# Four gated layers of cross attention and experts: routing by ScalarE, limits behind maxima, weights in the context's place, projections one ahead, two batches' keys first

## The chip, the cores and the metric

The kernel runs on one core of a Trainium2 chip. The metric is the device time of one execution in microseconds. A core has five engines with instruction queues of their own: TensorE (PE; PEld is its weight load), VectorE (DVE), ScalarE (ACT), GpSimd (POOL) and SyncE (SP), which here only issues DMAs. Each executes its queue in order; they meet through semaphores. Data lie in SBUF and PSUM with 128 partitions.

## The reference

`x` has 8 batches of 256 tokens of width 256, the context 8 batches of 256 tokens of width 192. Four layers each add a gated cross attention and a gated feed-forward part, on a layer norm of `x`:

```python
x = x + tanh(g_xattn[l]) * XATTN_l(layernorm(x), ctx)
x = x + tanh(g_ffn[l])   * FFN_l(layernorm(x))
```

- L0: the cosine of projected tokens and context in place of an attention; a feed-forward part in which only expert 0 counts.
- L1: softmax attention with 16 heads of 16, rows of padded tokens masked. FFN: 8 experts, each token takes its two best by gate logits (softmax over the two); `silu(x W1) * (x W2)` of width 682, then `W3`.
- L2: softmax attention with 16 heads of 64, then `w_o`. FFN: top 2 of 8 experts of width 256 by softmax scores plus a bias, and two shared experts.
- L3: 16 heads of 16 with clamped logits, `where(any(isnan(attn)), 1/Nkv, attn)`, then `Wo`:

```python
attn = einsum('bhqd,bhkd->bhqk', q, k) * scale
attn = softmax(clip(attn, -10000, 10000))
attn = where(any(isnan(attn)), 1.0 / Nkv, attn)
x = einsum('bhqk,bhkd->bqhd', attn, v) @ Wo + bo
```

  FFN: self attention over 256 tokens, in which a key mask splits tokens into two groups by their likeness to a guide vector; then a projection.

## The kernel before

The residual `x` stays in SBUF for the whole launch as 16 tiles of 128 tokens. The instruction order on each engine is made by the framework's scheduler at build time from the order in which the Python code issues operations; `behind(kind)` holds the next ones behind the last operation recorded under `latest[kind]`. PSUM is split in three large tiles (`psum2`, 2 x 512 floats) and two small ones (`psum1`).

**16-head attention** (`attention16`, in L1, L3 and L3's self attention). Work goes over batches b and four groups g of four heads. For a group, `greatest` makes logits (`lg`, eight matmuls of 32 rows in two `psum2` tiles) and their negated maxima over keys (`nms`, L641), with a clamp in L3 (L645). Every second group, `shift` transposes the maxima (`nt`) and adds them to the spare rows of the queries (L655). Three groups after `greatest`, `weights` makes the logits again, transposed and shifted (`lb`), and takes their exponential by ScalarE (`ex`; L1512 in L3). L3 then has `limits` (`limited`, L1518), by which VectorE clamps each exponential from below and above; the lower bound `low` of a half batch comes from ScalarE (`lowest`) and a broadcast DMA through DRAM. The limits are issued one group after the exponentials, and `values`, which multiplies the exponentials with the values, one group after that; `finish` transposes the result back. The next batch's `prologue` is a generator whose parts run beside these groups: mixing in the experts' results of the layer before (`x`, L1101), keys, values, norm (`xn`, L226), transposes (`xt`), queries. All loops are written in this order:

```python
                greatest(b, g)
            if late and 0 <= n - lag - 1 < n_all:
                limits(*divmod(n - lag - 1, 4))
```

After L3's attention, `copy_predicated` puts the mean in where a NaN was seen, and `out_projection` per batch transposes (`l3oNt`), copies by ScalarE (`l3oNT`, L762), multiplies with `Wo` (L769, in a `psum1` tile) and adds to `x` (L776).

**64-head-width attention** (`attention64`, L2) works in pairs of heads, with logits, exponentials, division, transposes (`et`) and values; `prologue(b)` makes batch b's mix, keys (`pk`), values (`pv`), norm and queries, four parts before the next batch's first pair.

**Experts.** `places` makes a list of tokens by expert from the mask of chosen experts. Each token has two places; slots hold 128 tokens of one expert, 39 slots in all. VectorE counts per expert (`own_n`, `run`, scan), TensorE sums over partitions (`pr`), VectorE gets places (`two`), then one-hot rows and columns (`row`, L966; `col`, L950; `what`, L955 and L958), TensorE multiplies them (`pi`, L971) and `token` (L977) is the list; `expert` is each slot's expert. `two_gates` picks the two gate weights of each token. `routed` then runs over slots: an indirect DMA gathers 128 tokens (`xg`, L1023), TensorE transposes them (`xt`, L1033), `value_load` puts the expert in a register, `first_half` multiplies with `w1` and `w2` (`ph`, L1129), `hidden_T` transposes the hidden layer (`ht`, L1050), `second_half` multiplies with `w3` (`po`, L1147). The weights of L1 take 17 MB in SBUF in three tiles: `l1_w1` is loaded early, `l1_w2` (5.5 MB) takes the place of earlier layers' weights (`w01_stack`) after L1's attention, `l1_w3` (6.1 MB in two DMAs) comes after it. Results go to DRAM by slot and are gathered back for each batch in the next layer's prologue (`combined`).

Of the kernel before, what the change touches and what calls it, by code (L numbers as in the profile page):

```python
# [15 lines left out]
P = 128  # L16
# [4 lines left out]
E = 8  # L21
# [14 lines left out]
def flamingo_kernel(ctx: ExitStack, tc: tile.TileContext, out: bass.AP, a: dict):  # L36
# [112 lines left out]
    def rows_of_halves(k, name, value=1.0):  # L149
# [9 lines left out]
    trip = const.tile([P, P], F32, name="trip")  # L159
    nc.gpsimd.memset(trip, 1.0)  # L160
    nc.gpsimd.affine_select(
        out=trip, in_=trip, compare_op=ALU.is_gt, fill=0.0, base=0,
        pattern=[[1, P]], channel_multiplier=-1,
# [216 lines left out]
    maxima = cleared_maxima(l1x1, "l1")  # L380

    def rows(b, k):

        if b == 0:
            return l1x1.tile([P, 4, S], F32, name=f"l1{k}0")
        return l1x.tile([P, 4, S], F32, tag=f"{k}T", bufs=3, name=f"l1{k}{b}")

    def l1_prologue(b):

        cx = ctx01[:, :, b * S : (b + 1) * S]  # L390
        with behind("maxima") if b else nullcontext():
            xn = layer_norm(b, f"l1x{b}", rowmask=maskf[:, 2 * b : 2 * b + 2])
        qT = rows(b, "q")
        kT = rows(b, "k")
        for _, pp in project(wk, 2, lambda c: cx[:, c, :], 2, f"l1pk{b}"):
            for u in range(2):
                nc.scalar.activation(
                    of_half(kT, u), pp[:, 0:2, :], AF.Identity,
                    bias=one_a[:, u : u + 1], scale=half[:, u : u + 1],
                )  # L400
        yield
        xnT = lnp.tile([P, 2, S], F32, tag="xnT", name=f"xnT_l1x{b}")
        transposed(xn, xnT, f"l1x{b}")
        yield
        for _, pp in project(wq, 2, lambda c: xnT[:, c, :], 2, f"l1pq{b}"):
            for u in range(2):
                nc.vector.tensor_scalar(
                    of_half(qT, u), pp[:, 0:2, :], quarter[:, u : u + 1], None, ALU.mult
                )
        yield  # L410
        va = vas[b % 3]
        values16(wv, lambda c, k: cx[:, c, k * P : (k + 1) * P], va, f"l1pv{b}")
        yield qT, kT, va

# [91 lines left out]

    def attention64(tag, pl, prologue, epilogue, lag=2):

# [72 lines left out]

        gens[0] = prologue(0)
        while 0 not in state:
            advance(0)
        for n in range(n_all + lag + 1):
            if n < n_all:
                b, p = divmod(n, npair)
                if p == 0 and b + 1 < B:
                    gens[b + 1] = prologue(b + 1)
                logits(b, p)  # L590
                advance(b + 1)
# [6 lines left out]
    def attention16(tag, pl, maxima, prologue, epilogue, mrow=16, lag=3, clamp=None,  # L598
# [73 lines left out]
        def limits(b, g):  # L672
            for p in (2 * g, 2 * g + 1):
                clamp[2](b, p, exs[b, p])
# [47 lines left out]
        for n in range(n_all + lag + 1 + late):  # L722
# [5 lines left out]
            if late and 0 <= n - lag - 1 < n_all:  # L728
                limits(*divmod(n - lag - 1, 4))
            if n < n_all:  # L730
# [16 lines left out]

    def out_projection(att, nf, w, gate, brow, b, pl, name, bufs=1):

        projected(out_transposed(att, nf, pl, name, bufs), nf, w, gate, brow, b, name)  # L750

    def out_transposed(att, nf, pl, name, bufs=1):
# [11 lines left out]

    def projected(attT, nf, w, gate, brow, b, name):
        po = psum1(f"{name}o")
        for i in range(2):
# [127 lines left out]

    w01_stack.close()


    def places(mask, name, pl1, kept):

        flat = mask.rearrange("p e t -> p (e t)")
        run = pl1.tile([P, E * NT], F32, name=f"{name}run")
        nc.vector.tensor_tensor_scan(run, ones[:, : E * NT], flat, 0.0, ALU.mult, ALU.add)
        nc.vector.tensor_sub(run, run, flat)
        own_n = pl1.tile([P, E], F32, name=f"{name}own_n")
        nc.vector.tensor_reduce(own_n, mask, AX.X, ALU.add)
        pr = psum1(f"{name}pr")
        nc.tensor.matmul(pr[:, P : P + E], ones, own_n, start=True, stop=True)  # L910
        nc.tensor.matmul(pr[:, 0:P], trip, flat, start=True, stop=False)
# [3 lines left out]
        n_i = pl1.tile([P, E], I32, name=f"{name}n_i")  # L915
        nc.vector.tensor_scalar_add(n_i, pr[:, P : P + E], float(P - 1))
        nc.vector.tensor_single_scalar(n_i, n_i, -P, ALU.bitwise_and)
        sizes = pl1.tile([P, 2, E], F32, name=f"{name}sizes")
        nc.vector.tensor_copy(sizes[:, 0, :], n_i)
        nc.vector.tensor_sub(sizes[:, 1, :], sizes[:, 0, :], pr[:, P : P + E])  # L920
        lower = pl1.tile([P, 2, E, E], F32, name=f"{name}lower")
# [32 lines left out]
        what = pl1.tile([P, 2 * NT, 2, SP], BF16, name=f"{name}what")  # L954
        nc.vector.tensor_scalar_mul(what[:, :, 0, :], col, own_p)  # L955
        for k in range(2):
            ts = slice(k * NT, (k + 1) * NT)
            nc.vector.tensor_tensor(  # L958
                what[:, ts, 1, :], col[:, ts, :],
                count[:, :NT].unsqueeze(2).to_broadcast([P, NT, SP]), ALU.mult,  # L960
            )
        pi = psum1(f"{name}pi")
        for k in range(4):
            ts = slice(k * NT // 2, (k + 1) * NT // 2)
            row = pl1.tile([P, NT // 2, P], BF16, tag=f"{name}row", name=f"{name}row{k}", bufs=2)
            nc.vector.tensor_tensor(  # L966
                row, count.unsqueeze(1).to_broadcast([P, NT // 2, P]),
                rc[:, 0, ts].unsqueeze(2).to_broadcast([P, NT // 2, P]), ALU.is_equal,
            )
            for t in range(k * NT // 2, (k + 1) * NT // 2):  # L970
# [3 lines left out]
                )  # L974
        part = pl1.tile([P, SP], F32, name=f"{name}part")
        nc.vector.tensor_copy(part, pi[:, 0:SP])
        nc.vector.scalar_tensor_tensor(token, pi[:, SP : 2 * SP], float(P), part, ALU.mult, ALU.add)  # L977

        at = pl1.tile([P, SP, E], F32, name=f"{name}at")
        edge = pl1.tile([P, E], F32, name=f"{name}edge")  # L980
        nc.vector.tensor_scalar_mul(edge, first[:, 0, :], 1.0 / P)
        nc.vector.tensor_tensor(
            at, edge.unsqueeze(1).to_broadcast([P, SP, E]),
            count[:, :SP].unsqueeze(2).to_broadcast([P, SP, E]), ALU.is_le,
        )
        expert_f = pl1.tile([P, SP], F32, name=f"{name}expert_f")
        nc.vector.tensor_reduce(expert_f, at, AX.X, ALU.add)
        nc.vector.tensor_scalar_add(expert, expert_f, -1.0)
        return slot, two
# [25 lines left out]

    def routed(xd, yd, token, expert, first_half, second_half, nf, pl, name, halfway=None):

# [3 lines left out]
        def gather(s):  # L1021
            xg = pl.tile([P, D], F32, tag="xg", name=f"{name}xg{s}", bufs=4)
            nc.gpsimd.indirect_dma_start(  # L1023
# [86 lines left out]
    with tc.tile_pool(name="l1w", bufs=1, side="right") as plw:  # L1110
        l1_w2 = plw.tile([P, E, 2, HID], F32, name="l1_w2")
        nc.sync.dma_start(out=l1_w2, in_=a["l1f_w12"][:, :, :, HID:])
        l1_w3 = plw.tile([P, E, NHC, D], F32, name="l1_w3")
        for e0 in range(0, E, 4):
            nc.sync.dma_start(out=l1_w3[:, e0 : e0 + 4], in_=a["l1f_w3"][:, e0 : e0 + 4])
        l1_w12 = (l1_w1, l1_w2)
        token, expert, two_i, g2 = l1_kept
        with tc.tile_pool(name="l1p", bufs=1, side="right") as plp:
            slot, two = places(l1_mask, "l1g", plp, l1_kept[:3])
            l1_gates(slice(NT - 2, NT), "l1g_last")  # L1120
            two_gates(l1_gate, slot, two, gf(1), g2, "l1g", plp)
        with tc.tile_pool(name="l1f", bufs=2, side="right") as pl:
# [30 lines left out]
            def halfway():  # L1153
# [6 lines left out]
            routed(  # L1160
                l1xd, l1yd, token, expert, first_half, second_half, NHC, pl, "l1", halfway
            )


# [4 lines left out]
    with l2x_pool, tc.tile_pool(name="l2x", bufs=2) as pl:  # L1169
# [62 lines left out]

        attention64("l2", pl, prologue, epilogue)

# [6 lines left out]
    with tc.tile_pool(name="l2r", bufs=1) as pl1, ExitStack() as l2s_stack:  # L1241
# [18 lines left out]
        with tc.tile_pool(name="l2p", bufs=1) as plp:  # L1260
            slot, two = places(mask2, "l2g", plp, l2_kept[:3])
            nc.vector.tensor_tensor(gate2, gate2, mask2.rearrange("p e t -> p t e"), ALU.mult)
            two_gates(gate2, slot, two, gf(2), g2, "l2g", plp)

# [73 lines left out]
        with tc.tile_pool(name="l2f", bufs=2) as pl:  # L1338
# [60 lines left out]

            routed(xd, yd, token, expert, first_half, second_half, 2, pl, "l2")  # L1400
    l2w_stack.close()
# [3 lines left out]
    with tc.tile_pool(name="l3x", bufs=2) as pl, tc.tile_pool(name="l3x1", bufs=1) as pl1:  # L1405
# [31 lines left out]
        def prologue(b):  # L1437
# [27 lines left out]
            values16(wv3, lambda c, k: cx[:, c, k * P : (k + 1) * P], va, f"l3pv{b}")  # L1465
            xn = norm_apply(b, stats, f"l3x{b}")
            xnT = lnp.tile([P, 2, S], F32, tag="xnT", name=f"xnT_l3x{b}")
            transposed(xn, xnT, f"l3x{b}")
            yield
            pm = psum1(f"l3pm{b}")  # L1470
# [64 lines left out]
        nc.vector.tensor_copy(bad_i, bad_all.to_broadcast([P, D]))  # L1535
        for b in range(B):
            for i in range(2):
                nc.vector.copy_predicated(atts[:, 2 * b + i, :], bad_i, vmean[:, b, :])
            out_projection(atts[:, 2 * b : 2 * b + 2, :], 2, wo3, gx(3), None, b, pl, f"l3o{b}", bufs=2)

# [319 lines left out]
```

## Time and profile before

| | |
|---|---|
| median of 3 runs | 2044.46 us (2040.42 to 2046.01) |
| profiled execution | 2039.29 us, its span 2037.6 us |
| mean granted TensorE clock | 0.96 |
| L1 attention | 197 to 395 us of the span |
| L1 routing, up to the first gathered slot | 395 to 433 |
| L1 experts | 433 to 772 |
| L2 attention, its start included | 772 to 1206 |
| L2 router, shared experts, routing, experts | 1206 to 1447 |
| L3 attention, out-projections | 1447 to 1726, 1726 to 1755 |
| L3 self attention | 1755 to 2037.6 |

The profile is of one execution. A line of a group gives source line, engine, operation, output and inputs, count, then busy time and mean duration of one, then how long the engine had been idle just before these instructions and on what it waited. In a window's line each engine has its busy time and its instructions in brackets. Ends of matmuls are modelled, so sums of their durations overlap.

### The profile page before, as it was taken

Reading aid. Unit: us, or ns where it says so; the run is one execution under the profiler, and the core shown is the slowest. Engines: PE = TensorE matmul, PEld = TensorE weight load, DVE = VectorE, ACT = ScalarE, POOL = GpSimd, SP = SyncE. Lnnn points to the kernel's source line nnn. Section 1 sums busy time; section 2 is a strip of 40 time slices with the busy share of each in tenths; the row PEclk is TensorE's granted clock in tenths of the full one; section 3 lists DMA queues with packets and bytes.
Section 4 is the critical chain, followed back from the end, with each engine's and each line's share of the span. In section 5 each row is a group of like instructions: output and inputs, shape, how many; then the busy total and the mean of one; then the engine's idle time right before and its main releaser. Section 6 shows DMA issues by size and latency. Waiting matters only on the chain. (4 is left out here: it accounts for less than half of the span.)

```text
span 2037.6 us, 31056 instructions
## 1 busy us (share of the span) xinstructions
PE 1878.3 (92%) x12226; PEld 1237.3 (61%) x12226; DVE 1093.0 (54%) x2193; ACT 684.6 (34%) x1467; POOL 292.0 (14%) x324
## 2 busy tenths in 40 slices
PE   6999999859999998999999999999789898899998
PEld 5666666536666665566666665666555554675665
DVE  4534777631111113766666776333468777547763
ACT  2321444412221122433434432022254544234444
POOL 2421000011111101101111101033212110610000
PEclk8999999979999999999999999999889988999999
DMA  8000000151110114000000003023223221000000
GB/s 265 3 0 0 1 15 12 69 206 32 32 32 32 29 35 172 17 16 17 17 17 15 15 11 122 11 81 88 79 83 101 89 74 64 0 1 6 12 12 16
DMA packets 44285, 96.67 MB, mean 47 GB/s; under 512 B 6992, under 2 KB 30256, under 8 KB 40816
## 3 DMA queue, kind: packets, MB, share of 16 engines
q1 hardware_dynamic: 34736, 75.25, 10.4%
q0 software_dynamic: 6816, 18.62, 3.3%
q8 instruction: 100, 1.64, 0.3%
q10 hardware_dynamic: 2592, 0.82, 0.2%
q14 instruction: 41, 0.34, 0.1%
HBM read 78.02 MB, written 16.65 MB: 46 GB/s over the span
## 5 line engine op out<-in xcount | busy, mean ns | idle before, releaser
L1129 PE MATMUL l1ph<-l_w,l1xT 128*128 x624 | 191.0, 459 | 0.0
L537 ACT ACTIVATE l2ex<-l2lg,l2nm 128x256 f32<-128x256 f32 x256 | 118.1, 473 | 204.5 <-DVE l2nm L533 201.0
L1129 PEld LDWEIGHTS l1ph<-l_w,l1xT 128*128 128x128 f32 x624 | 115.9, 191 | 66.7 <-issue 13.6
L1139 DVE TENSOR_TENSOR l1h<-l1sl,l1ph 128x682 f32<-128x682 f32 x39 | 33.8, 866 | 175.1 <-PE l1ph L1129 170.3
L1147 PE MATMUL l1po<-l_w,l1hT 128*128 x468 | 121.1, 388 | 0.0
L1518 DVE SCALAR_TENSOR_TENSOR l3ex<-l3ex,l3low 128x1024 f32<-128x1024 f32 x64 | 75.8, 1225 | 49.7 <-ACT l3ex L1512 39.0
L641 DVE TENSOR_REDUCE l1nms<-l1lg 128x4 f32<-128x1024 f32 x64 | 75.5, 1221 | 43.7 <-PE l1lg L622 43.7
L641 DVE TENSOR_REDUCE l3nms<-l4lg 128x4 f32<-128x1024 f32 x64 | 75.4, 1220 | 40.2 <-PE l4lg L622 40.2
L1147 PEld LDWEIGHTS l1po<-l_w,l1hT 128*128 128x128 f32 x468 | 79.7, 189 | 19.8 <-issue 13.3
L533 DVE TENSOR_REDUCE l2nm<-l2lg 128x4 f32<-128x1024 f32 x64 | 78.0, 1219 | 21.3 <-PE l2lg L527 20.5
L1137 ACT ACTIVATE l1sl<-l1ph 128x682 f32<-128x682 f32 x39 | 28.9, 741 | 167.0 <-PE l1ph L1129 167.0
L557 DVE COPY l2et<-l2tp 128x512 f32<-128x512 f32 x128 | 83.4, 682 | 2.6 <-PE l2tp L553 2.5
L641 DVE TENSOR_REDUCE l3nms<-l3lg 128x4 f32<-128x1024 f32 x64 | 75.4, 1219 | 10.2 <-PE l3lg L622 10.1
L622 PE MATMUL l3lb<-l3q,l3k 32*128 32x256 f32 x512 | 63.9, 452 | 18.1 <-DVE l3nms L641 16.5
L542 DVE TENSOR_TENSOR l2ex<-l2ex,l2z 128x1024 f32<-128x1024 f32 x64 | 78.1, 1221 | 1.5
L1023 POOL DMA_INDIRECT l1xg<-l1xd,l1token x39 | 37.3, 956 | 282.1 <-PE l1xt L1033 255.3
L527 PE MATMUL l2lg<-l2k,l2q 64*128 64x256 f32 x512 | 76.5, 402 | 0.4 <-ACT l2ex L537 0.4
L1512 ACT ACTIVATE l3ex<-l3lb 128x1024 f32<-128x1024 f32 x64 | 64.8, 1018 | 34.3 <-PE l3lb L622 34.3
L667 ACT ACTIVATE l4ex<-l4lb 128x1024 f32<-128x1024 f32 x64 | 61.9, 1020 | 41.0 <-PE l4lb L622 40.6
L667 ACT ACTIVATE l1ex<-l1lb 128x1024 f32<-128x1024 f32 x64 | 62.0, 1022 | 40.1 <-PE l1lb L622 39.2
L572 PE MATMUL l2av<-l2et,l2va 128*32 128x256 f32 x1024 | 74.4, 385 | 0.0
L553 PE MATMUL l2tp<-ident,l2ex 128*128 128x128 f32 x512 | 71.2, 279 | 3.4 <-DVE l2et L557 2.8
(745 smaller groups left out, 3757.4 us busy)
## 6 DMA issues: line engine op xcount, KB each, us to landing
l3low<-low_d SPq DMA_DIRECT2D x16, 1024.0 KB
l_w<-in_l1f_w SPq DMA_DIRECT2D x2, 5456.0 KB
l_w<-in_l1f_w SPq DMA_DIRECT2D x2, 3072.0 KB
l1yd<-l1y SPq DMA_DIRECT2D x39, 128.0 KB
l2yd<-l2y SPq DMA_DIRECT2D x39, 128.0 KB
l_w<-in_l2f_w SPq DMA_DIRECT2D x1, 4096.0 KB
x<-in_x SPq DMA_DIRECT2D x8, 256.0 KB
w_l0f_w<-in_l0f_w SPq DMA_DIRECT2D x2, 1024.0 KB
```

What stands on the lines that cost most here:

```text
L527: nc.tensor.matmul(lg[:, j, i * S : (i + 1) * S], qT[r, p, i * P : (i + 1) * P], kT[r, p, :], start=True, stop=True,)
L533: latest["maxima"] = nc.vector.tensor_reduce(nm, lgv, AX.X, ALU.max, negate=True)
L537: nc.scalar.activation(ex[:, k, :], lgv[:, k, :], AF.Exp, bias=nm[:, k : k + 1], accum_out=z[:, k : k + 1],)
L542: nc.vector.tensor_tensor(ex, ex, z.unsqueeze(2).to_broadcast([P, 4, S]), ALU.mult)
L553: nc.tensor.transpose(tp[:, o : o + P], ex[:, 2 * j + i, k * P : (k + 1) * P], ident)
L557: nc.vector.tensor_copy(et, tp.rearrange("p (k n) -> p k n", k=2))
L572: nc.tensor.matmul(av[32 * j : 32 * j + 32, p % 4, :], va[:, k, 2 * p + j // 2, 32 * (j % 2) : 32 * (j % 2) + 32], pair[j // 2][:, k, :], ...
L641: latest["maxima"] = nc.vector.tensor_reduce(dst, lgv, AX.X, ALU.max, negate=True)
L667: nc.scalar.activation(exf, lbf, AF.Exp)
L1129: nc.tensor.matmul(ph[k][:, n, :HH], xT[:, c, :], l1_w12[k][:, bass.ds(e, 1), c, o : o + HH].rearrange("p o n -> p (o n)"), start=c == 0, ...
L1147: nc.tensor.matmul(po, hT[:n, f, :], l1_w3[:n, bass.ds(e, 1), f, :].rearrange("p o n -> p (o n)"), start=f == 0, stop=f == NHC - 1,)
L1518: nc.vector.scalar_tensor_tensor(exv, exv, 1.0, low.unsqueeze(1).to_broadcast([P, 2, 2 * S]), ALU.min, ALU.max)
```

## The change

- `places`: the count `own_n` is made first and gets a PSUM tile of its own (`pn`); `run - flat` goes into the constant `trip` (fill −1); ScalarE makes `what`, in 17 activations; `row` has four buffers; `token` is one reduction; the expert list is issued behind `token` (L1) or the rows (L2), and so are the gates.
- `l1_w2` is opened and loaded in the prologue of L1's last batch.
- `routed` takes the gathered tiles `xg` from a pool that is opened earlier.
- L1's rows of keys and queries have named tiles by `b % 3`.
- `attention64` can begin with four parts of batches 0 and 1 (`first_parts=4` in L2).
- In L3, `limits` is issued behind the maxima, `xn` too, and `xn`'s transposes one part later.
- L3's out-projections: batch b's transposes and copy are issued ahead of batch b−1's matmuls, whose result takes a `psum2` tile; the copies have three buffers.

```diff
@@ constants
-    nc.gpsimd.memset(trip, 1.0)
+    nc.gpsimd.memset(trip, 0.0)
     nc.gpsimd.affine_select(
-        out=trip, in_=trip, compare_op=ALU.is_gt, fill=0.0, base=0,
+        out=trip, in_=trip, compare_op=ALU.is_gt, fill=-1.0, base=0,
...
@@ l1_prologue(b)
         values16(wv, lambda c, k: cx[:, c, k * P : (k + 1) * P], va, f"l1pv{b}")
+        if b == B - 1:
+            w01_stack.close()
+            pool = l1w2_stack.enter_context(tc.tile_pool(name="l1w2", bufs=1, side="right"))
+            l1_w2.append(pool.tile([P, E, 2, HID], F32, name="l1_w2"))
+            nc.sync.dma_start(out=l1_w2[0], in_=a["l1f_w12"][:, :, :, HID:])
...
@@ attention64
-        gens[0] = prologue(0)
+        for b in range(2 if first_parts else 1):
+            gens[b] = prologue(b)
+            for _ in range(first_parts):
+                advance(b)
...
@@ attention16
             if late and 0 <= n - lag - 1 < n_all:
-                limits(*divmod(n - lag - 1, 4))
+                with behind("maxima"):
+                    limits(*divmod(n - lag - 1, 4))
...
@@ projected
-        po = psum1(f"{name}o")
+        po = psum2(f"{name}o")[:, 0, :] if wide else psum1(f"{name}o")
...
@@ places
+        own_n = pl1.tile([P, E], F32, name=f"{name}own_n")
+        nc.vector.tensor_reduce(own_n, mask, AX.X, ALU.add)
         run = pl1.tile([P, E * NT], F32, name=f"{name}run")
         nc.vector.tensor_tensor_scan(run, ones[:, : E * NT], flat, 0.0, ALU.mult, ALU.add)
-        nc.vector.tensor_sub(run, run, flat)
...
+        pn = psum1(f"{name}pn")
+        nc.tensor.matmul(pn[:, 0:E], ones, own_n, start=True, stop=True)
         pr = psum1(f"{name}pr")
-        nc.tensor.matmul(pr[:, P : P + E], ones, own_n, start=True, stop=True)
...
-        nc.vector.tensor_scalar_mul(what[:, :, 0, :], col, own_p)
-        for k in range(2):
-            ts = slice(k * NT, (k + 1) * NT)
-            nc.vector.tensor_tensor(
-                what[:, ts, 1, :], col[:, ts, :],
-                count[:, :NT].unsqueeze(2).to_broadcast([P, NT, SP]), ALU.mult,
-            )
+        nc.scalar.activation(what[:, :, 0, :], col, AF.Copy, scale=own_p)
+        what_t = what.rearrange("p (k t) w s -> p k t w s", k=2)
+        col_t = col.rearrange("p (k t) s -> p k t s", k=2)
+        for t in range(NT):
+            nc.scalar.activation(
+                what_t[:, :, t, 1, :], col_t[:, :, t, :], AF.Copy, scale=float(t * P)
+            )
...
-            row = pl1.tile([P, NT // 2, P], BF16, tag=f"{name}row", name=f"{name}row{k}", bufs=2)
-            nc.vector.tensor_tensor(
+            row = pl1.tile([P, NT // 2, P], BF16, tag=f"{name}row", name=f"{name}row{k}", bufs=4)
+            latest["rows"] = nc.vector.tensor_tensor(
...
-        part = pl1.tile([P, SP], F32, name=f"{name}part")
-        nc.vector.tensor_copy(part, pi[:, 0:SP])
-        nc.vector.scalar_tensor_tensor(token, pi[:, SP : 2 * SP], float(P), part, ALU.mult, ALU.add)
+            latest["token"] = nc.vector.tensor_reduce(
+                token, pi[:, : 2 * SP].rearrange("p (k s) -> p s k", k=2), AX.X, ALU.add
+            )
...
+        with behind(rest):
+            nc.vector.tensor_scalar_mul(edge, first[:, 0, :], 1.0 / P)
...
+            nc.vector.tensor_reduce(expert_f, at, AX.X, ALU.add)
+            nc.vector.tensor_scalar_add(expert, expert_f, -1.0)
...
@@ routed
-            xg = pl.tile([P, D], F32, tag="xg", name=f"{name}xg{s}", bufs=4)
+            xg = plg.tile([P, D], F32, tag="xg", name=f"{name}xg{s}", bufs=4)
...
@@ L1 experts
-            slot, two = places(l1_mask, "l1g", plp, l1_kept[:3])
-            l1_gates(slice(NT - 2, NT), "l1g_last")
-            two_gates(l1_gate, slot, two, gf(1), g2, "l1g", plp)
+            slot, two = places(l1_mask, "l1g", plp, l1_kept[:3], "token")
+            with behind("token"):
+                l1_gates(slice(NT - 2, NT), "l1g_last")
+                two_gates(l1_gate, slot, two, gf(1), g2, "l1g", plp)
...
@@ L2 attention, L2 experts
-        attention64("l2", pl, prologue, epilogue)
+        attention64("l2", pl, prologue, epilogue, first_parts=4)
...
-            slot, two = places(mask2, "l2g", plp, l2_kept[:3])
+            slot, two = places(mask2, "l2g", plp, l2_kept[:3], "rows")
...
@@ L3 prologue
-            xn = norm_apply(b, stats, f"l3x{b}")
+            with behind("maxima") if b else nullcontext():
+                xn = norm_apply(b, stats, f"l3x{b}")
+            yield
             xnT = lnp.tile([P, 2, S], F32, tag="xnT", name=f"xnT_l3x{b}")
             transposed(xn, xnT, f"l3x{b}")
-            yield
...
@@ behind L3's attention
-        for b in range(B):
-            for i in range(2):
-                nc.vector.copy_predicated(atts[:, 2 * b + i, :], bad_i, vmean[:, b, :])
-            out_projection(atts[:, 2 * b : 2 * b + 2, :], 2, wo3, gx(3), None, b, pl, f"l3o{b}", bufs=2)
+        attTs = {}
+        for b in range(B + 1):
+            if b < B:
+                for i in range(2):
+                    nc.vector.copy_predicated(atts[:, 2 * b + i, :], bad_i, vmean[:, b, :])
+                attTs[b] = out_transposed(atts[:, 2 * b : 2 * b + 2, :], 2, pl, f"l3o{b}", bufs=3)
+            if b > 0:
+                projected(attTs.pop(b - 1), 2, wo3, gx(3), None, b - 1, f"l3o{b - 1}", wide=True)
```

## The prediction

> **What bounds the kernel now.** I read the busy shares first, then windows by stage, then in each touched stage the groups by line and the timeline.
>
> Layers are called L0 to L3. Busy shares, and windows for L1's routing, L1's experts, L2's routing, the steady part of L3's cross attention and its out-projections (columns: PE, PEld, DVE, ACT, POOL busy, granted TensorE clock, DMA share, GB/s):
>
> ```profile
> PE 1878.3 (92%) x12226; PEld 1237.3 (61%) x12226; DVE 1093.0 (54%) x2193; ACT 684.6 (34%) x1467; POOL 292.0 (14%) x324
> ```
> ```profile
> 395.00:433.00 38.00, 9.06 (x61) 6.92 (x59) 22.22 (x76) 2.30 (x4) 4.85 (x5) 0.56 0.85 334
> 433.00:772.00 339.00, 334.41 (x1400) 228.03 (x1400) 62.98 (x116) 68.03 (x156) 33.15 (x35) 0.99 0.13 40
> ...
> 1271.00:1281.00 10.00, 5.74 (x43) 4.43 (x43) 7.21 (x15) 0.00 (x0) 1.75 (x3) 0.66 0.00 1
> ...
> 1525.00:1720.00 195.00, 175.10 (x1476) 103.51 (x1480) 145.99 (x234) 94.74 (x184) 27.21 (x26) 0.89 0.24 86
> 1720.00:1755.00 35.00, 25.11 (x153) 17.98 (x144) 27.26 (x72) 7.82 (x15) 7.81 (x10) 1.00 0.00 1
> ```
>
> TensorE sets the time nearly everywhere, so only its holes can be won: the 38 us routing hole (29 us of it idle), the 10 us hole, and the last attention, where it is idle 20 us and the clock is 0.89. The groups there:
>
> ```profile
> L1518 DVE SCALAR_TENSOR_TENSOR l3ex<-l3ex,l3low 128x1024 f32<-128x1024 f32 x50 | 59.0, 1222 | 37.9 <-ACT l3ex L1512 35.3 <-DMA l3low<-low_d 2.6
> L641 DVE TENSOR_REDUCE l3nms<-l3lg 128x4 f32<-128x1024 f32 x47 | 55.3, 1219 | 0.1
> ...
> L622 PE MATMUL l3lb<-l3q,l3k 32*128 32x256 f32 x428 | 52.6, 445 | 15.8 <-DVE l3nms L641 14.8 <-ACT l3ex L1512 0.4
> ```
>
> VectorE stands 35.3 us at the limits, waiting for ScalarE's exponentials, while the maxima that TensorE needs are queued behind: maxima themselves wait 0.1 us, so their logits were long there. TensorE then waits 14.8 us for them, since logits of both kinds share the three large PSUM tiles.
>
> **L3 attention: limits behind the maxima.** Starts of successive shifts give six batch lengths of 30.52, 31.02, 31.36, 32.36, 36.52 and 30.63 us, mean 32.07. I count VectorE's work of a batch by start-to-start steps in the timeline: 8 maxima and 8 limits at 1.13, 8 clamps at 0.12, four mixes at 0.40, two shifts at 0.65, about 3.0 of statistics, normalization and division: 25 us. TensorE's: logits 1.36, biased logits 1.43 and values 1.07 in each of four groups, 15.4; keys 1.9, queries 1.9, values 1.15, transposes 2.8, mean 0.6: about 24. In the layer-1 attention the same matmuls have 24.4 us per batch.
>
> The new order puts maxima, clamp, limit, clamp, limit in each group. The exponentials (two of 1.02) now run on ScalarE during 2.27 us of maxima, so no limit waits for them; the values that read a limit come a group later on TensorE. What stays is logits that come late. Group by group from the end T of the logits: keys 1.9, transposes 0.6, biased logits 1.43, values 1.07 and the first logits 0.68 give T+5.7, where VectorE is through at T+4.7: 1.0 us idle. In the group with the mix VectorE needs about 8 us, TensorE 4.2, so TensorE waits 3.9. In the last, the transposes of xn are moved next to the queries: xt 0.6, its copy 0.59, queries 1.9, biased logits 1.43, values 1.07 put the next logits about 1.2 us behind VectorE. Sum 25+1.0+1.2 = 27.2, with one more crossing 27.4. Bounds are 25 (VectorE alone) and 32.07 (nothing won).
>
> A gap also costs clock. After an idle 1.18 us the timeline shows 12 biased logits in 2.08 us, where full speed gives 12/16 of 1.43, 1.07:
>
> ```profile
> 1593.69 0.70 PE L622 MATMUL l3lb<-l3q,l3k 32*128 32x256 f32 x4 [1.18 <-DVE l3nms L641]
> ...
> 1594.82 2.08 PE L622 MATMUL l3lb<-l3q,l3k 32*128 32x256 f32 x12 [0.43 <-DVE l3nms L641]
> ```
>
> By clock 0.89, 21 us of full-speed work were lost in this window, with no gap over 2.2 us. The mix group keeps a gap, so I allow 1 us more: 28.4. Gain 3.67 × 6 = 22 us (0 to 29). [...]
>
> **L1 routing.** The mask is ready at 406.37, the token list at 424.78, the first gather starts 0.98 later and its transpose runs at 432.16, 7.4 us behind the list. Own counts, kept in a PSUM tile of their own, come 1.4 us earlier (VectorE no longer scans first). About 1.4 us of interleaved gate and expert work moves behind the token. Weights of the rows leave VectorE (0.55 + 2×0.82) for ScalarE: no row shows these; copies of 128x256 and 128x512 take 0.37 and 0.59, so one of 128x80 takes 0.17 to 0.25 and one of 128x1280 about 1.25, together 4 to 5.3. Beside them VectorE makes four rows (4×1.15), no longer held to two buffers. Ten expert loads of 0.69 us that stand ahead of TensorE's routing matmuls go behind. I get the list at 418.4 to 419.7, 5 to 6.4 us earlier. Then the gather: 5.46 MB of w2 were issued at 398.36 and with w3 kept the queues full to 431:
>
> ```profile
> l_w<-in_l1f_w SPq DMA_DIRECT2D x2, 3072.0 KB
> l_w<-in_l1f_w SPq DMA_DIRECT2D x1, 5456.0 KB
> ```
>
> At 400 GB/s w2 is 13.6 us. It now goes out in the last attention batches (DMA share 0.03 there) behind the release of the old weights; on SP only the write of l1xd5 is queued behind it. So w3 ends at about 414, and a gather without neighbours, as those of 789.6 to 793.6, lands 2.4 us after issue instead of 6.4. Together 5+4 to 6.4+4, less 0.5 for loads that now stand between the first transposes: I take 9 us (5, with the list alone, to 11). The gate chain of 4.1 us now follows the token and covers the gather; it ends about when xT is copied.
>
> **L1 expert slots.** The expert list now comes behind the token, so its register loads cannot run ahead. Before, 22 were loaded in the hole. TensorE starts a slot every 8.48 us in slots 2 to 25, and every 8.94 us in 26 to 38 (one 9.29), which load their own. There an output matmul is also moved behind the last hidden transposes, which then wait:
>
> ```profile
> L1050 PE MATMUL l1ht<-ident,l1h 128*128 128x128 f32 x76 | 13.1, 281 | 3.6 <-DVE l1xT L1035 3.6
> ```
>
> The new order gives slots from 6 on what those slots have: 20 × 0.46 = **+9.2 us** (8 to 10). This takes back the hole's gain.
>
> **L2 attention begins with two batches' keys and values.** The 4.35 us wait for xn of batch 0 (785.56 to 789.90) is filled, but by 12.9 us of TensorE work ahead of it. Batch 1's mix enters VectorE ahead of the key copies and waits for gathers landing at 795.95; TensorE needs those copies' PSUM, about 5 us idle to 800.3. Later, batch 0 has less filler against 3.9 us of VectorE a pair (3.5 on TensorE). I take 0 (−2 to +2.5).
>
> **L2 routing.** TensorE's gaps are 1.29+1.53+0.77+0.67 = 4.3, with 6.8 us at half clock. The same edits end the list about 4 us earlier (1274.3 for 1278.4). Here slots step 3.02 us with or without their own expert load. Gain 4 (1.5 to 5.5).
>
> **L3 out-projections.** Each waits for its own attT copy: seven gaps of 0.68 to 0.73 and one of 2.37, in which xn of the next stage holds up VectorE's residual:
>
> ```profile
> L769 PE MATMUL l3o1o<-w_l3x_wo,l3o1T 128*128 128x256 f32 x8 | 2.0, 392 | 0.7 <-ACT l3o1T L762 0.7
> ...
> L769 PE MATMUL l3o4o<-w_l3x_wo,l3o4T 128*128 128x256 f32 x8 | 2.0, 388 | 2.4 <-DVE x L776 2.4
> ```
>
> One batch ahead, the copy (0.59) lies under 2.0 us of matmul, and the result's tile is one of three. One copy stays open, with part of VectorE's crossing: gain 5 (3 to 6.5). The rest (the trip constant, tiles by b%3) moves no order: 0.
>
> **Sum.** −9 + 9.2 + 0 − 4 − 22 − 5 = −30.8. The profiled execution took 2039.29 (span 2037.6), so 2008.5; the median shown, 2044.46, is 5.2 above it, so **2013.7** for a median, rounded to 2014.
>
> **Rivals.**
> 1. The query chain sets the L3 pace. xn is behind the maxima and its transposes beside the queries. If the xn copy waits in ScalarE's line behind two exponentials (2.0) and avT (0.58), the next logits are 3.1 us later, the pace 30.5 with a half-clock stretch left in, and the gain 9: 2027. For it: TensorE has nothing else to do there. Against: exponentials of that group precede xn's matmuls.
> 2. Slower: VectorE and TensorE take turns in L3. Maxima ahead of limits block VectorE whenever logits aren't there, and values block TensorE until limits are through. If each of four groups exposes biased logits, values and the first logits (1.43+1.07+0.68, less 0.3), VectorE's 25 becomes 36.5, +4.4 × 6 = +26 instead of −22: 2044.5 − 8.8 + 26 = 2062. It decides once values need limits of their own group; the order has one group between, and the three PSUM tiles are the one narrow place.
> 3. ScalarE's routing is no shorter. At the 0.45 us step of its 128x256 activations, 16 take 7.2 us; the lists come 2.5 us later each, hole gain 6.5 and L2's 1.5: 2014 + 5 = 2019.
> 4. Order gives nothing in L3 (half-clock stretches re-form at the mix): 2014 + 22 = 2036, faster by 0.4%.
>
> **Numbers.** The forecast 0.52, rivals 1: 0.18, 2: 0.08, 3: 0.12, 4: 0.10. A measurement here tells about 0.3%, 6.1 us. Half of 4 falls within that, and some of 1: same 0.08; slower is 2 and a little of 4: 0.10; faster 0.82. The range begins at 2001 (L3 gain 28, hole 11, L2 5.5, out-projection 6.5) and reaches to 2038 over rival 4; what lies above is 2.
>
> **What would show it.** L3 batch lengths near 28; limits' idle for l3ex from 35 to under 5 us; clock above 0.89. First l1xt at 421 to 425. l1ht waiting for l1xT in all slots and a slot step of 8.94 from slot 6 on; 8.48 there would make me wrong by 9 us. Out-projection gaps gone. Batch lengths above 31 would make the forecast wrong.

## The result, and the profile after

The changed kernel takes 2032.96 us (median of 20 runs, 2026.97 to 2042.7) where the kernel before takes 2045.24 (20 runs): ratio 0.9942, with a 95% interval of 0.9926 to 0.9958. It is faster by 0.6%, 12 us, where 30.8 were forecast. The profiled execution took 2032.9 (span 2031.2) against 2039.29 (2037.6).

Stage by stage, from marks in the two traces (us):

| stage | before | after | difference | forecast |
|---|---|---|---|---|
| L1 routing: last value matmul to first gathered transpose | 38.3 | 28.7 | −9.6 | −9 |
| L1 experts: from there to the last output matmul | 340.7 | 350.2 | +9.5 | +9.2 |
| L2 attention: from there to its last value matmul | 440.2 | 441.6 | +1.5 | 0 |
| L2 routing: from there to the token list | 65.9 | 64.3 | −1.6 | −4 |
| L3 attention: first logits to first out-projection transpose | 263.5 | 262.8 | −0.7 | −22 |
| L3 out-projections: from there to the next stage's transposes | 26.8 | 17.8 | −9.0 | −5 |
| from there to the self attention's logits | 65.0 | 68.2 | +3.2 | 0 |

The windows of the changed kernel that answer to those shown of before (columns: PE, PEld, DVE, ACT, POOL busy, granted clock, DMA share, GB/s):

```profile
395.00:424.00 29.00, 9.86 (x60) 7.57 (x59) 20.96 (x71) 4.92 (x20) 4.56 (x5) 0.59 0.60 237
424.00:773.00 349.00, 338.65 (x1404) 228.25 (x1405) 62.99 (x116) 69.06 (x157) 33.54 (x36) 1.00 0.12 41
1271.00:1281.00 10.00, 9.23 (x57) 5.68 (x56) 8.77 (x18) 4.40 (x18) 1.43 (x1) 1.00 0.00 0
1525.00:1720.00 195.00, 163.83 (x1440) 100.57 (x1438) 146.03 (x233) 94.09 (x181) 25.66 (x26) 0.90 0.24 85
1726.00:1744.00 18.00, 17.76 (x101) 15.61 (x99) 16.39 (x54) 4.59 (x8) 5.38 (x6) 1.00 0.00 1
```

The routing hole is 9 us shorter, the out-projections leave TensorE idle 0.2 of 18 us. L3's attention has the clock of before, 0.90 for 0.89, and TensorE is busy less of it, not more (163.83 of 195 us for 175.10). Its groups (line numbers have moved: the limits are L1535, the maxima L657, both kinds of logits L638, the exponentials L1529, the shift L671, the row of lower bounds L1514):

```profile
L1535 DVE SCALAR_TENSOR_TENSOR l3ex<-l3ex,l3low 128x1024 f32<-128x1024 f32 x52 | 62.9, 1219 | 6.0 <-ACT l3ex L1529 6.0
L657 DVE TENSOR_REDUCE l3nms<-l3lg 128x4 f32<-128x1024 f32 x46 | 54.1, 1220 | 41.3 <-PE l3lg L638 41.3
...
L638 PE MATMUL l3lg<-l3k,l3q 32*128 32x256 f32 x368 | 38.4, 427 | 11.6 <-ACT l3ex L1529 11.0 <-DVE l3atts L800 0.6
```

The line of the first logits in the kernel before, over the same window:

```profile
L622 PE MATMUL l3lg<-l3k,l3q 32*128 32x256 f32 x368 | 40.6, 460 | 3.2 <-ACT l3ex L1512 2.4 <-DVE l3atts L786 0.8
```

The edit did what it says: limits no longer stand waiting for exponentials (6.0 us for 35.3). But VectorE now stands 41.3 us at the maxima, waiting for logits, and TensorE's logits wait 11.0 us for exponentials, which they did for 2.4 before. The timeline of one batch shows the chain (start, duration, engine, line, operation; in brackets the idle time before it and its releaser):

```profile
1538.54 1.22 DVE L1535 SCALAR_TENSOR_TENSOR l3ex<-l3ex,l3low 128x1024 f32<-128x1024 f32 x1
...
1539.75 1.22 DVE L1535 SCALAR_TENSOR_TENSOR l3ex<-l3ex,l3low 128x1024 f32<-128x1024 f32 x1
1540.88 0.73 DVE L226 TENSOR_SCALAR xn_l3x<-x,mv_l3x,rp_l3x 128x256 f32<-128x256 f32 x2
1541.53 0.69 DVE L671 TENSOR_TENSOR l3q<-l3nt,l3q 128x512 f32<-128x512 f32 x1
...
1542.27 0.66 PE L241 MATMUL xt_l3x<-ident,xn_l3x 128*128 128x128 f32 x4 [1.28 <-DVE l3q L671]
1542.30 0.72 ACT L1514 ACTIVATE l3lowr<-l3q,minus_clamp 128x512 f32<-128x512 f32 x1 [2.56 <-issue]
1542.93 1.00 ACT L1529 ACTIVATE l3ex<-l3lb 128x1024 f32<-128x1024 f32 x1
...
1543.92 0.57 ACT L709 COPY l3avT<-l3av 128x512 f32<-128x512 f32 x1
...
1544.55 2.08 PE L1489 MATMUL l3pm<-l3va,mean 128*128 128x256 f32 x4 [1.62 <-ACT l3avT L709]
...
1546.42 3.62 PE L359 MATMUL l3pq<-xnT_l3x,w_l3x_wq 128*128 128x256 f32 x8
...
1553.85 2.36 DVE L657 TENSOR_REDUCE l3nms<-l3lg 128x4 f32<-128x1024 f32 x2 [6.96 <-PE l3lg L638]
```

The shift of the queries stands behind two limits and xn on VectorE. ScalarE's row of lower bounds needs the shifted queries and holds up ScalarE's queue until 1542.30, 0.08 us behind the shift's end; behind it wait an exponential and the copy avT; avT holds one of the two small PSUM tiles, which the mean needs (it waits 1.62 us for avT). Then the granted clock is 0.51 from 1543.4 to 1550.3: the queries take 3.62 us for 1.9, and VectorE waits 6.96 us for the next batch's logits.

### The profile page after: what moved, and what is told of

It reads as the page before. It is cut to its first block, busy times and chain, and to the rows that moved or that the text cites. A ratio compares the mean times of both kernels' runs of the same rounds, so it can differ in the third digit from the quotient of the medians.

```text
span 2031.2 us, 31093 instructions
## 1 busy us (share of the span) xinstructions
PE 1872.4 (92%) x12226; PEld 1237.7 (61%) x12226; DVE 1086.4 (53%) x2183; ACT 690.9 (34%) x1501; POOL 290.2 (14%) x324
## 5 line engine op out<-in xcount | busy, mean ns | idle before, releaser
L1142 PEld LDWEIGHTS l1ph<-l_w,l1xT 128*128 128x128 f32 x624 | 115.5, 190 | 66.7 <-issue 13.5
L1152 DVE TENSOR_TENSOR l1h<-l1sl,l1ph 128x682 f32<-128x682 f32 x39 | 33.8, 867 | 174.7 <-PE l1ph L1142 169.9
L657 DVE TENSOR_REDUCE l3nms<-l3lg 128x4 f32<-128x1024 f32 x64 | 75.4, 1219 | 59.5 <-PE l3lg L638 59.5
L657 DVE TENSOR_REDUCE l1nms<-l1lg 128x4 f32<-128x1024 f32 x64 | 75.5, 1221 | 43.7 <-PE l1lg L638 43.7
L657 DVE TENSOR_REDUCE l3nms<-l4lg 128x4 f32<-128x1024 f32 x64 | 75.4, 1220 | 40.2 <-PE l4lg L638 40.2
L1535 DVE SCALAR_TENSOR_TENSOR l3ex<-l3ex,l3low 128x1024 f32<-128x1024 f32 x64 | 77.4, 1219 | 9.8 <-ACT l3ex L1529 7.4
L1529 ACT ACTIVATE l3ex<-l3lb 128x1024 f32<-128x1024 f32 x64 | 64.8, 1019 | 44.0 <-PE l3lb L638 44.0
L1080 DVE COPY l1y<-l1po 128x256 f32<-128x256 f32 x39 | 16.6, 425 | 110.7 <-PE l1po L1160 110.7
L566 PEld LDWEIGHTS l2tp<-ident,l2ex 128*128 128x128 f32 x512 | 56.0, 141 | 30.4 <-issue 12.7
```

The costliest lines, as they stand in the source:

```text
L566: nc.tensor.transpose(tp[:, o : o + P], ex[:, 2 * j + i, k * P : (k + 1) * P], ident)
L657: latest["maxima"] = nc.vector.tensor_reduce(dst, lgv, AX.X, ALU.max, negate=True)
L1142: nc.tensor.matmul(ph[k][:, n, :HH], xT[:, c, :], l1_w12[k][:, bass.ds(e, 1), c, o : o + HH].rearrange("p o n -> p (o n)"), start=c == 0, ...
L1529: nc.scalar.activation(exf, lbf, AF.Exp, accum_out=sums[:, col : col + 1])
L1535: nc.vector.scalar_tensor_tensor(exv, exv, 1.0, low.unsqueeze(1).to_broadcast([P, 2, 2 * S]), ALU.min, ALU.max)
```

## Experiments

All start from the changed kernel. The theory after the two traces, A: in L3 the limits stand not only behind the maxima but ahead of the shift and of xn, and others wait for these. Rivals: the late xn alone eats the gain (B), or the half clock does in any order (C).

**xn early.** The first part of the edit on xn undone:

```diff
-            with behind("maxima") if b else nullcontext():
-                xn = norm_apply(b, stats, f"l3x{b}")
-            yield
+            xn = norm_apply(b, stats, f"l3x{b}")
             xnT = lnp.tile([P, 2, S], F32, tag="xnT", name=f"xnT_l3x{b}")
             transposed(xn, xnT, f"l3x{b}")
+            yield
```

> The changed kernel, with xn and its transposes of L3 in their old places (xn not held behind the maxima, transposes one part earlier); limits stay behind the maxima. L3 from its first logits to the first out-projection transpose took 263.5 us before and 262.8 after. Theory A (limits now stand ahead of the shift of the queries and of xn on VectorE; ScalarE's lower-bound row and its exponentials wait for the shift, TensorE for xn, the mean and the queries): this takes away the waits for xn only, stage about 253 to 257. Rival B (the late place of xn and its transposes alone eats the gain): stage about 238 to 243, batches of 28 to 29 us. Rival C (the clock falls to half in any order, the pace cannot change): stage 261 to 264.

L3 took 275.7 us, and the kernel 2050.14, ratio 1.0032 (1.001 to 1.0055): slower than before. A, B and C all missed. The late xn is not the cost; in this order of the limits it wins 13 us. The groups of this run, 1525 to 1720:

```profile
L1534 DVE SCALAR_TENSOR_TENSOR l3ex<-l3ex,l3low 128x1024 f32<-128x1024 f32 x48 | 58.2, 1218 | 0.0
L657 DVE TENSOR_REDUCE l3nms<-l3lg 128x4 f32<-128x1024 f32 x48 | 56.5, 1220 | 51.2 <-PE l3lg L638 51.2
...
L638 PE MATMUL l3lg<-l3k,l3q 32*128 32x256 f32 x372 | 42.0, 460 | 18.9 <-ACT l3ex L1528 18.3 <-DVE l3atts L800 0.5
```

With limits ahead of the shift and xn as before, logits wait 18.3 us for exponentials: the loss is in the limits' place.

**Limits as before, xn late.**

```diff
-                with behind("maxima"):
-                    limits(*divmod(n - lag - 1, 4))
+                limits(*divmod(n - lag - 1, 4))
```

> The changed kernel, with L3's limits issued as before (not held behind the maxima); xn and its transposes stay late. Theory A: limits wait again for exponentials ahead of the maxima (idle of the limits near 35 us), the late xn adds its wait: stage 264 to 270 us against 262.8. Rival B: the late xn costs as much as the limits' place won, so the stage goes to 280 or more. Rival C: 261 to 264.

L3 took 253.4 us, the kernel 2023.87, ratio 0.9904 (0.9866 to 0.9942). Again none of the three: without the limits' move L3 is 9 us shorter than with it. The two halves of the L3 edit work against each other: by these single profiles the limits' place costs 9 to 12 us, and the late xn wins 10 to 13.

**Limits behind the shift.** What A should have led to: the maxima first, then the shift, where a group has one, then the limits; xn early.

```diff
-            if late and 0 <= n - lag - 1 < n_all:
-                with behind("maxima"):
-                    limits(*divmod(n - lag - 1, 4))
...
                 shift(b, g // 2)
+            if late and 0 <= n - lag - 1 < n_all:
+                with behind("shift" if n % 2 == 0 and n <= n_all else "maxima"):
+                    limits(*divmod(n - lag - 1, 4))
```

> The changed kernel, with L3's limits issued after the shift of the queries where a group has one, behind the maxima where not, and xn and its transposes in their old places. Theory A: neither ScalarE's row nor TensorE's queries wait behind limits; VectorE sets the pace at 27.5 to 29 us a batch, stage 238 to 248, the whole 15 to 25 us below the changed kernel, ratio to before about 0.984. Rival B: like the run with xn early, no better. Rival C: stage 261 to 264.

L3 took 233.3 us, less than the 238 to 248 that A gave, and the kernel 2003.47, ratio 0.9791 (0.9761 to 0.9822). Five of its batches last 28.2 us each. From 1525 to 1690:

```profile
L657 DVE TENSOR_REDUCE l3nms<-l3lg 128x4 f32<-128x1024 f32 x46 | 54.1, 1219 | 14.5 <-PE l3lg L638 14.5
...
1525.00:1690.00 165.00, 153.31 (x1407) 92.00 (x1396) 147.89 (x229) 91.29 (x178) 28.55 (x26) 0.98 0.28 95
```

VectorE is busy 147.9 of 165 us and its wait for logits is 14.5; the clock is 0.98, for 0.92 over the same window in the changed kernel. C is out: the half clock went with the waits, nothing was done against it directly. A second execution of the same kernel:

> The same kernel as the run with limits after the shift and xn early, once more for its stage times: L3 233 us within 2 us, if the stage follows from the order and not from the execution.

L3 took 230.2 us; the kernel 2007.03. The stage follows from the order, with an execution's spread of 3 us (expected within 2).

**The row behind the exponentials.** Limits stay ahead of the shift. In the two traces VectorE's L3 instructions stand in the same order; on ScalarE only the row has another place:

```diff
             if clamp is not None:
-                clamp[0](b, half, qh)
+                held.append((b, half, qh))
...
                 weights(*divmod(n - lag, 4))
+            while held:
+                with behind("exponentials") if "exponentials" in latest else nullcontext():
+                    clamp[0](*held.pop())
```

> The changed kernel, with ScalarE's row for the lower bounds in L3 (which needs the shifted queries) issued behind the two exponentials of its group; limits stay between maxima and shift. Theory A2 (ScalarE's queue: the row waits for the shift that now stands behind the limits, and the exponentials, whose PSUM tiles TensorE needs for the next logits, wait behind the row): the 1.80 us wait of logits for exponentials and the 1.62 us wait of the mean go, with some of the half clock; L3 from first logits to the first out-projection transpose 236 to 248 us against 262.8. Rival D (the delay runs through the shift itself: transposed logits need the shifted queries, so TensorE waits with any order on ScalarE): 258 to 264.

L3 took 238.8 us, the kernel 2012.05, ratio 0.9845 (0.9801 to 0.9889). From 1525 to 1690:

```profile
L657 DVE TENSOR_REDUCE l3nms<-l3lg 128x4 f32<-128x1024 f32 x45 | 53.0, 1220 | 25.4 <-PE l3lg L638 25.4
...
L638 PE MATMUL l3lg<-l3k,l3q 32*128 32x256 f32 x352 | 35.0, 409 | 3.6 <-ACT l3ex L1532 3.0 <-DVE l3atts L803 0.6
```

The logits' wait for exponentials is 3.0 us, for 11.0 in the changed kernel. So the delay runs through ScalarE's queue: the 0.72 us row, waiting for the shift, kept exponentials back that needed nothing but their logits. Against the changed kernel's profile, taking it out of the way brings 24 us, and limits behind the shift 29.5. Rival D is out.

**Limits behind the shift, xn late as in the change** (the third experiment's edit without the one on xn).

> The changed kernel, with L3's limits issued after the shift of the queries where a group has one; xn and its transposes stay late, as in the change. With limits ahead of the shift a late xn won 13 us (275.7 to 262.8), with limits as before 10 us. Theory A2 (the late xn wins because it gives the shift and the clamps an earlier place on VectorE): with the shift ahead anyway nothing is left to win, 228 to 236 us as with xn early (233.3 and 230.2). Rival (the late xn wins by itself, since its TensorE transposes then don't stand between logits): 218 to 226.

L3 took 229.7 us, the kernel 2002.6, ratio 0.9808 (0.9767 to 0.985): with the shift ahead, xn's place makes no difference beyond the spread. Why it won 10 us with the limits as before is not settled. In the traces it goes with the clock: from 1525 to 1690 that is 0.96 in the run with the limits as before, and 0.90 in the kernel before, whose batches take 30.5 to 36.5 us where that run's take 30.4 to 31.3. Why it falls less often there is not shown.

**L1's expert list not behind the token list.**

```diff
-        with behind(rest):
+        with behind(rest) if rest == "rows" else nullcontext():
             nc.vector.tensor_scalar_mul(edge, first[:, 0, :], 1.0 / P)
```

> The changed kernel, with L1's expert list not held behind the token list, so that TensorE loads 16 of its registers before the slots, ten of them ahead of or between the routing matmuls. If the register load in a slot (and the order that comes with it) makes the 8.94 us step: the step is 8.48 in some 15 more slots, 6.9 us less in the experts, the routing 0 to 2 us longer, so 5 to 7 us less in all against the changed kernel. Rival (the step comes from another thing, the place of the weights or DMA traffic): 8.94 stays and nothing is won.

The experts took 343.6 us for 350.2 (8.48 us steps in 15 more slots), the routing 30.5 for 28.7: 4.8 us won, a little under the 5 expected. The kernel took 2027.68, ratio 0.9914 (0.9883 to 0.9945). The last hidden transposes don't wait in this run's slots that step 8.48 us (460 to 580), and wait in the changed kernel's that step 8.94 (460 to 651):

```profile
L1064 PE MATMUL l1ht<-ident,l1h 128*128 128x128 f32 x84 | 14.2, 278 | 0.0
```
```profile
L1064 PE MATMUL l1ht<-ident,l1h 128*128 128x128 f32 x128 | 22.2, 282 | 6.1 <-DVE l1xT L1049 6.1
```

So the load in the slot, with the order that comes with it, makes the step; the run does not part the two.

**One batch's parts first in L2** (`attention64` without `first_parts=4`).

> The changed kernel, with L2's attention beginning with one batch's parts as before. From the end of L1's last expert matmul to the last value matmul of L2's attention before took 440.2 us, the changed kernel 441.6. If the two batches' keys cost what the traces show: 440 to 440.5, 1 to 1.5 us less than the changed kernel. Rival (they gain, and another edit costs): 443 or more.

From L1's last output to L2's last value matmul: 440.3 us against 441.6, within 440 to 440.5. This settles little: the stage took 439.6 to 442.6 us (mean 441.2) in the eleven executions that begin with two batches, and 440.2 to 440.8 (mean 440.4) in the three that begin with one. A price of about 1 us is likely and not shown. The kernel took 2029.56, ratio 0.9947 (0.9925 to 0.9969), which doesn't tell 1 us either.

**Out-projections as before.**

```diff
-            if b > 0:
-                projected(attTs.pop(b - 1), 2, wo3, gx(3), None, b - 1, f"l3o{b - 1}", wide=True)
+            attT = out_transposed(atts[:, 2 * b : 2 * b + 2, :], 2, pl, f"l3o{b}", bufs=2)
+            projected(attT, 2, wo3, gx(3), None, b, f"l3o{b}")
```

> The changed kernel, with L3's out-projections as before (each batch's transposes right ahead of its matmuls, two buffers, small PSUM tile). From its first transpose to the first logits of the self attention took 91.8 us before and 86.1 in the changed kernel. If the order alone did it: 91 to 92. Rival (the earlier end of VectorE's work before the stage does it): 86 to 88.

From its first transpose to the self attention's first logits: 26.8 + 64.9 = 91.7 us, and the kernel takes 2038.98, ratio 0.998 (0.9959 to 1.0001). So the edit itself (order, PSUM tile and buffers together) wins 9 us in its stage, and not the earlier end of VectorE's work. The 3.2 us that the stage behind it lost in the changed kernel's profile are mostly spread: that stage took 64.2 to 69.3 us, mean 66.0, in the eleven other executions that have the new out-projections, and 65.0 and 64.9 in the two that have the old. A price of 1 us can't be excluded.

**w2 behind the attention.** Two runs; the edit of the second:

```diff
-        if b == B - 1:
-            w01_stack.close()
...
+    w01_stack.close()
...
+        l1_w2.append(plw.tile([P, E, 2, HID], F32, name="l1_w2"))
+        nc.sync.dma_start(out=l1_w2[0], in_=a["l1f_w12"][:, :, :, HID:])
```

> The changed kernel, with L1's w2 opened and loaded behind the attention as before; all else of the routing stays changed. From the last value matmul of L1's attention to the first gathered transpose took 38.3 us before, 28.6 to 28.7 in the changed kernel. If the gather shares its queues with w2 and w3 again: the list is ready as early as in the changed kernel, the gather lands some 7 us behind its issue instead of 2.4 and the routing takes 32 to 34 us; with all of it queued behind both loads (to 431 us of the span) up to 37. Rival (the gather's time does not depend on w2): 28 to 29.

Nothing follows from this run: the load was written behind the attention, but the scheduler kept it at 359.4 us, and the routing took 28.7. In the second run the tile is taken from w3's pool, so that it has to wait:

> The changed kernel, with L1's w2 opened in the same pool as w3, behind the attention, as before; in the run before this one the load had kept its early place (issued at 359 us), so that run says nothing on it. Here it stands on SyncE's queue between the last writes of L1's tokens and w3. From the last value matmul of L1's attention to the first gathered transpose: 32 to 34 us if the gather shares its queues with w3 to the end (landing some 7 us behind its issue, as before, instead of 2.4), against 28.7; w3's end, near 431, must also delay the first output matmuls no further. Rival (the gather's landing does not depend on w2): 28 to 29.

The routing took 34.4 us, a little above the 32 to 34 expected, with the list as early as in the changed kernel (418.75, there 418.34). The first gather, and what the transposes wait for, in this run and in the changed kernel:

```profile
419.64 1.31 POOL L1032 DMA_INDIRECT l1xg<-l1xd,l1token  x1 [19.08 <-DVE l1gate L844]
...
428.68 0.66 PE L1042 MATMUL l1xt<-ident,l1xg 128*128 128x128 f32 x2 [10.21 <-DMA l1xg<-l1xd,l1token]
```
```profile
419.23 1.31 POOL L1037 DMA_INDIRECT l1xg<-l1xd,l1token  x1 [19.08 <-DVE l1gate L850]
...
422.51 0.66 PE L1047 MATMUL l1xt<-ident,l1xg 128*128 128x128 f32 x2 [4.45 <-DMA l1xg<-l1xd,l1token]
```

From the start of the gather to the transpose 9.0 us beside the weights' load, 3.3 without it. Of the 9.6 us that routing won, 5.8 go with w2's early load; the shorter list alone keeps 3.9.

**Combined:** limits behind the shift (xn late), the expert list first, one batch first in L2.

> The changed kernel, with three of its edits mended by what the runs showed: L3's limits behind the shift of the queries (xn late as in the change), L1's expert list not held behind the token list, one batch's parts first in L2. By stages: L3 230 us against 259, experts and routing 4.8 less, L2's start 1.1 less. Against the changed kernel's 0.9942 of before that is 35 us, 1.7%, less: 1996 to 2000 us where before takes 2045, ratio 0.976 to 0.979. Rival (stages give each other back what they win): no faster than the run with limits behind the shift alone, 0.979 to 0.981.

2000.91 us, ratio 0.9771 (0.9756 to 0.9786), L3 233.6, routing and experts 374.1 against 378.8. That is inside the ratio expected and a little above the time; its interval overlaps that of the limits behind the shift alone, so that of the small edits only the expert list's gain of 4.8 us is shown, by its stages and not by the total.

## Why the prediction was wrong

**L3, the failing step.** The sum took 22 us for the limits' move. In the profile 0.7 came; over six executions with this L3 order (the changed kernel and five of the runs above) the stage took 257.9 to 262.8, mean 259.5, so about 4 us against the one of before. The step that failed is "What stays is logits that come late", with its 1.0 and 1.2 us: it followed VectorE's order of maxima, clamps and limits and TensorE's matmuls, and did not ask where the shift then stands and who waits for it. The shift stands behind the limits, ScalarE's row waits for it at the head of ScalarE's queue, and the exponentials, the logits and the maxima wait behind the row. VectorE's wait for logits is about 6.9 us a batch (41.3 of 195 us, at 32.35 us a batch), where the sum has 2.2. In the run with the row behind the exponentials the stage takes 24.7 us less than in the kernel before, so the forecast gain is there.

The other terms held in the run with limits behind the shift: VectorE is busy 25.3 us a batch (147.9 of 165 us at 28.2), 25 forecast, and waits 2.5 for logits. That its pace of 28.2 us is so near the forecast 28.4 is partly luck, since 1 us of the 28.4 was for half clock and the clock there is 0.98. In the changed kernel the clock won nothing, 0.90 for 0.89. The range's low end has 28 us for L3, 6 × (32.07 − 27.4) without the 1 us for half clock: no run of this order shows it (0.7 to 5.6 us won), and with the limits behind the shift the stage takes 29.9 to 33.8 us less. The batch lengths of the changed kernel, above 31 us in five of seven, are what the text had named as making it wrong.

**Rival 1** had the right place, the queries of the next batch behind ScalarE's queue, and its 2027 is near the 2033 measured. Its mechanism was half right: the copies wait, but behind a row that waits for the shift, and the late xn that it blamed wins time. Rival 4 (nothing won in L3, half clock comes back) gave 2036, nearest to the measured time, and is right that the clock stays at 0.90; but that goes with this order's waits, since with the limits behind the shift the clock is 0.98. Rival 2 (2062, values waiting for limits) did not come: TensorE's value matmuls have no wait in the changed kernel from 1525 to 1720. The run with xn early is slower than before, but by logits that wait for exponentials. Rival 3 is out: the 16 activations take 2.6 us, not 7.2.

**L1.** Both terms held: 9 forecast and 9.6 measured, 9.2 and 9.5; the list came 6.4 us earlier (5 to 6.4 forecast), the gather took 3.3 us to its transpose instead of 6.4. While w2's early load ran, the core's DMA moved 402 GB/s (361.6 to 373.9), where the sum has 400 for w2. They don't simply add: without w2's early load only 3.9 us of the earlier list are left, since the gather then takes 9.0 us to its transpose beside the weights. **Out-projection:** 5 forecast, 9 measured. Of the 7.4 us of gaps only 0.24 is left, at the first copy, so that VectorE's crossing, which I left open, went too; the other 1.8 us are less busy time of TensorE, 17.6 for 19.4, which the sum did not have. **L2's start:** 0 forecast, +1.5 in the profile, which is within the spread of this stage; a 6.1 us wait is at the place forecast. **L2 routing:** from the mask to the list 16.9 us became 12.1, as worked out (4), but the mask itself came 3 us later, beside 6.8 us at a clock of 0.50 (below); the stage won 1.6, and in the executions without the stretch, at 61.1 us, 4.8.

The profiled execution of before was 6 us under the median of its 20 runs, that of the changed kernel at its median; this is the rest of the way from 6.4 us between the profiled executions to 12.3 between the medians.

## What to carry to other kernels

When an operation is moved back in one engine's queue, list everything that it now precedes, and for each who waits for that on a third engine, and what stands behind the waiter in its queue. Here 0.72 us of work on ScalarE, behind the shift, kept TensorE's logits waiting: 11.0 us for exponentials, 3.0 with the row behind them. An order with two halves should be tried half by half: by single profiles the halves were worth −10 and +9 us, and a third place for the limits 30.

## What was not expected of the hardware

The same L2 stage, from the last value matmul to the token list, took 61.1, 64.3, 65.9 or 67.6 us in executions with the same instructions there. TensorE's granted clock and busy time go with it, and VectorE's, ScalarE's and GpSimd's busy times differ by 0.12 us at most (the executions with limits behind the shift, and with one batch first):

```profile
1215.50:1283.10 67.60, 65.47 (x256) 39.38 (x256) 34.08 (x79) 19.63 (x40) 10.89 (x29) 0.90 0.28 100
```
```profile
1215.20:1276.30 61.10, 58.94 (x256) 34.81 (x256) 34.20 (x79) 19.63 (x40) 10.89 (x29) 1.00 0.31 110
```

In the changed kernel (64.3 us) TensorE has gaps of 0.72 and 0.68 us up to 1222.56 and 1224.78; the granted clock is 0.50 from 1226.0 to 1232.8, and 1.00 ahead of it and behind it in the stage (1214.3 to 1278.6). Beside these 6.8 us at half speed the stage takes 3.2 us longer than 61.1. For 65.9 us (the run with the old out-projections) and 67.6, the mean clocks of 0.92 and 0.90 give by my estimate about 10.5 and 13.5 us at half speed, beside 4.8 and 6.5 us more; in the runs with xn early and with one batch first, 61.1 us, the clock is 1.00. So the half speed comes and goes with the same instructions there.

That a gap costs clock, as the prediction has it, does not hold for every gap: the kernel before has the same two, 0.72 and 0.68 us up to 1221.26 and 1223.48, and its clock is 1.00 from 1223 to 1240. Whether the gaps do it in the changed kernel is not shown: between them TensorE runs transposes and matmuls with 8 columns (L241 and L818).
